# Letting the first gathers of a graph-attention kernel wait for TensorE's table of K and V

## The chip, the cores and the metric

The kernel runs on one core of one Trainium2 chip. The metric is device time in microseconds (us) of one execution. Three runs of the kernel before took 2426.94, 2427.33 and 2434.01 us; their median is 2427.33 us. One more execution was profiled, and every duration below that isn't one of these three is from that profile.

## What is computed

The reference is one layer of graph attention with a residual and a normalization. Nodes N = 6250, edges E = 206250 (sorted by `dst`), D = 128 columns, 8 heads of 16:

```python
Kh, Qh, Vh = x @ WK, x @ WQ, x @ WV            # per node, 8 heads x 16
Eh = edge_attr @ WE                            # per edge
score = einsum('ehd,ehd,ehd->eh', Kh[src], Qh[dst], Eh) / 4
score = exp(clip(score, -5, 5))
wV = segment_sum(Vh[src] * score[:, :, None], dst)
Z = segment_sum(score, dst)
out = layernorm(x + wV / (Z[:, :, None] + 1e-6))
```

All inputs are float32. `Kh[src]` and `Vh[src]` are the costly part: a row of 256 floats for each of 206250 edges, from addresses that only `src` knows.

## The kernel before

The edges are cut into 1612 tiles of 128, and the tiles into 406 batches, nearly all of four tiles. A batch's K and V rows come to SBUF through four indirect DMAs ("gathers", one for each tile, line 314 in `gather`), all issued by GpSimd (POOL). Batches from 12 on (`XB = 12`) gather 1 KB rows of a table `kv` in HBM, which holds K and V of every node. The first twelve don't need this table: they gather the 512-byte rows of `x` itself (48 gathers), and TensorE makes K and V of those rows on the spot (`project`, lines 323 to 335: transposes `xtps`, copies `xgT`, matmuls `kvps`). So the kernel has work while the table is being made. There are 17 buffers for gathered batches (`GB`).

The table is made by `table(b0)`, line 226, called 13 times for groups of four blocks of 128 nodes, 49 blocks in all. For each block TensorE does one float32 matmul of 128x256 (line 232, `kvacc`) into a PSUM bank. Four banks are used in turn, so a block's matmul waits until the block four places ahead has been copied out. The copy to the SBUF tile `kvst` is ScalarE's for even blocks (line 237) and VectorE's for odd ones (line 235). A finished group goes to `kv` in one store of 512 KB on SyncE's queue (line 240); `kvst` has two buffers, so a group's first copies wait for the store of two groups before. The last block of 106 rows has a store of its own (line 245). Every gather from `kv` comes after all of these stores have landed.

Up to batch 11 the instructions of each engine stand where a scheduler put them; from batch 12 on they stand as the loop at line 464 issues them. TensorE's queue holds blocks 0 to 11 of the table, two matmuls of `qrows` (line 258, the table of Q), blocks 12 to 27, one `qrows`, blocks 28 to 35, one `qrows`, blocks 36 to 43, one `qrows`, twelve transposes `xtps` of batches 0 to 2, and blocks 44 to 48; then batch 0 begins (`kvps` line 334, `eps` line 358, `qps` line 354, `pps` line 373, `agg` line 431). Each of these float32 matmuls is two matmul instructions with two weight loads in the trace, so a block of the table is four TensorE records; a transpose is two.

GpSimd's queue holds the 48 gathers of x first and then those of `kv`. Each gather waits for the eighth gather before it (eight semaphores are used in turn) and for its buffer. The first gather of `kv` waits for the stores of the table as well. From batch 16 (`LOCK`) the first gather of batch b also waits for the `qps` matmul of batch b - lag(b), where the lag falls from 12 to 1 within 44 batches and stays there (lines 303 to 320). Batches 0 to 15 have no such wait.

```python
gathered = {b: gather(b) for b in range(min(XB, len(batches)))}   # line 446
for b0 in range(0, NB, KB):                                       # NB = 49, KB = 4
    table(b0)
```

Of the kernel before, what the change touches and what calls it, by code (L numbers as in the profile page):

```python
# [15 lines left out]
P = 128  # L16
# [5 lines left out]
LEFT, RIGHT = 43, 128  # L22
# [6 lines left out]
XB = 12  # L29
# [19 lines left out]
def cut_batches():  # L49
    out, t = [], 0  # L50
    while t < NT:
        k = B
        if t >= NT - TAIL:
            k = 2 if NT - t > 3 else 1
        out.append(range(t, t + k))
        t += k
    return out
# [17 lines left out]
def q_built(j):  # L75

    return min(NB, (j * N // NJ + 3 * P - 1) // P)
# [3 lines left out]
def edge_attention(ctx: ExitStack, tc: tile.TileContext, x, xT, srcT, dstT, dstB, dst0, bnd, lo, eaT,  # L81
                   wq, wkv, we, out, kv, qtab, qs, relD):
    nc = tc.nc
# [6 lines left out]
    wkv_sb = cp.tile([D, 2 * D], F32, name="wkv_sb")  # L90
    nc.scalar.dma_start(wkv_sb, wkv)
    xT_sb = cp.tile([P, XC], F32, name="xT_sb")
# [16 lines left out]
    def src_col(t):  # L109
        return src_sb[0][:, t:t + 1] if t < C0 else src_sb[1][:, t - C0:t - C0 + 1]  # L110

    with ExitStack() as fast:
# [32 lines left out]
        def count(rows, cl, vals, hi):  # L145

            nc.vector.tensor_scalar(cl, vals, 0.0, float(hi), op0=ALU.max, op1=ALU.min)
            nc.vector.tensor_tensor(cl, cl, vals, op=ALU.is_equal)
            nc.vector.tensor_reduce(cn[:rows, len(counts):len(counts) + 1], cl, axis=AX.X, op=ALU.add)
            counts.append(rows)  # L150

        def from_window(i):

            a, k = i * P, min(P, NJ - i * P)
            if i == len(dB_sb):
                dB_sb.append(ip.tile([P, WT * P], I32, name="dB_sb", bufs=1))
                nc.sync.dma_start(dB_sb[i][:k], dstB[a:a + k])
            d = dB_sb[i]
            w = ip.tile([P, 1], F32, name="wq0", bufs=2)
            nc.vector.tensor_tensor(w[:k], d[:k, :1], bnd_c[:k, i:i + 1], op=ALU.min)  # L160
            r = ip.tile([P, WT * P], BF16, name="relq", bufs=1)
            nc.vector.tensor_scalar(r[:k], d[:k], w[:k], None, op0=ALU.subtract)
            nc.sync.dma_start(relD[a:a + k], r[:k])
            cl = wp.tile([P, WT * P], F32, name="clq", tag="kvst", bufs=2)
            count(k, cl[:k], r[:k], QW - 1)
# [52 lines left out]
        def pair_bank(i, name, shape):  # L218

            pool, tag = ((psE, "eps"), (psP, "pps"), (psQ, "qps"), (psP, "pps"))[i % 4]  # L220
            return pool.tile(shape, F32, name=name, tag=tag)


        KB = 4

        def table(b0):
            st = wp.tile([P, KB, 2 * D], F32, name="kvst", bufs=2)
            blocks = range(b0, min(NB, b0 + KB))
            for b in blocks:
                n = min(P, N - b * P)  # L230
                ps = pair_bank(b, "kvacc", [P, 2 * D])
                nc.tensor.matmul(ps[:n], xT_sb[:, LEFT + b * P:LEFT + b * P + n], wkv_sb,
                                 start=True, stop=True)
                if b % 2:
                    nc.vector.tensor_copy(st[:n, b - b0, :], ps[:n])
                else:
                    nc.scalar.copy(st[:n, b - b0, :], ps[:n])
            full = [b for b in blocks if (b + 1) * P <= N]
            if full:
                nc.sync.dma_start(  # L240
                    kv[b0 * P:(b0 + len(full)) * P].rearrange("(b p) f -> p b f", p=P),
                    st[:, :len(full), :])
            if len(full) < len(blocks):
                b = blocks[-1]
                nc.sync.dma_start(kv[b * P:N], st[:N - b * P, b - b0, :])

        batches = cut_batches()
        nbat = len(batches)
# [38 lines left out]
        chunks, aggs, sums, st8, expanded = {}, {}, {}, {}, {}  # L287

        def load_chunk(c):
            if c in chunks or c * CH >= NT:  # L290
                return
            n = min(CH, NT - c * CH) * P
            tl = ep.tile([P, CH * P], F32, name="ea")
            nc.sync.dma_start(tl[:, :n], eaT[:, c * CH * P:c * CH * P + n])
            chunks[c] = tl
# [7 lines left out]
        def lag(b):  # L303

            return max(STEP, 12 - (b - LOCK) // 4)

        def gather(b):
            rows, f = (x, D) if b < XB else (kv, 2 * D)
            g = gp.tile([P, B, 2 * D], F32, name="kvrows")
            for i, t in enumerate(batches[b]):  # L310
                k = min(P, (E - t * P + 63) // 64 * 64)
                if k < P:
                    nc.vector.memset(g[k:, i, :], 0.0)
                ins = nc.gpsimd.indirect_dma_start(  # L314
                    out=g[:k, i, :f], out_offset=None, in_=rows,
                    in_offset=bass.IndirectOffsetOnAxis(ap=src_col(t)[:k], axis=0))
                if i == 0 and b >= LOCK:
                    tc.add_manual_dep(ins.ins, expanded[b - lag(b)].ins.name,
                                      mybir.DependencyInfo(mybir.DependencyClass.Sync, mybir.DependencyReason.DATA),
                                      reason="gathers keep to TensorE's pace")  # L320
            return g
# [96 lines left out]
        def stage_c(b):  # L418
            n, g, oh, m = st8.pop(b)
            for i in range(n):  # L420
# [18 lines left out]
                elif last:  # L439
# [3 lines left out]
                    if k[1] == 0 and k[0] > 0:  # L443
                        ready.append(k[0] - 1)

        gathered = {b: gather(b) for b in range(min(XB, len(batches)))}
        for b0 in range(0, NB, KB):
            table(b0)
            if b0 == 2 * KB:
                load_chunk(0)  # L450
        from_window(0)
        for q in range(q_built(QLOOK + 2)):
            q_rows(q)
# [10 lines left out]
        for b in range(nbat + 4):  # L464
# [6 lines left out]
            if b < nbat:  # L471
                load_chunk(batches[b][0] // CH + EB - 3)
                load_rel(batches[b][0] // RC + 1)
                load_q(batches[b][0] // WT + QLOOK)
                g = gathered.pop(b) if b in gathered else gather(b)
                if b == min(XB, nbat - 1):
                    late_loads()
                if b == min(XB + 8, nbat - 1):
                    relative(C0, NT)
                if b == 14:  # L480
                    from_window(1)
                if b == 0:
                    for i in range(AHEAD):
                        stage_0(i)
                if b > 0:
                    turn(b - 1)
                stage_a(b, g)
            elif b == nbat:
                turn(b - 1)
# [178 lines left out]
```

## Time and profile before

| what | value |
|---|---|
| median of three runs | 2427.33 us |
| the profiled execution's own time | 2430.0 us |
| its span, first to last instruction | 2428.1 us |
| mean granted TensorE clock | 0.811 |
| gathers of x: first starts, last ends | 3.39 us, 63.73 us |
| `kvst` copies of the table: first, last start | 8.4 us, 88.1 us |
| last store of the table is issued | 90.33 us |
| first gather of `kv` | 96.25 us |
| first and last `qps` of batches 0 to 60 | 91.3 us, 413.8 us |

A row of the profile's groups names line, engine, operation and tiles, then the count, busy time and mean duration, then the idle time just before and what ended most of it. In the table of windows each engine's cell is its busy time and, in brackets, the number of its records; PEld is TensorE's weight loads. In a timeline the first two numbers are start and busy time, and the square bracket holds the engine's idle time before the instruction and what ended it. "remote" and "another core or an unknown queue" stand where the profile has no record of what released a wait at that time; there is only one core here.

### The profile page before, as it was taken

To read this page: it belongs to the slowest core of one execution; us is meant where nothing else is said; L and a number is where in the kernel's file an instruction comes from. 1 tells how busy PE (TensorE), PEld (TensorE's weight loads), DVE (VectorE), ACT (ScalarE), POOL (GpSimd) and SP (SyncE) were. 2 spreads that over 40 slices of the span, in tenths; PEclk is the share of its full clock that TensorE was granted. 3 is DMA by queue.
4 is the path that set the end of the run, shared out by engine and by line. 5 is a ranking of instruction groups with operands and counts; after the bars stand their busy time and mean duration, and the time that the engine had idled before them with its cause. 6 is when DMAs were issued, how large, how long until landed. Compare 5 with 4: busy or idle time off the path is not lost.

```text
span 2428.1 us, 24930 instructions
## 1 busy us (share of the span) xinstructions
PE 1539.8 (63%) x6880; PEld 1086.0 (45%) x6880; DVE 1577.4 (65%) x3779; ACT 458.9 (19%) x1572; POOL 1534.0 (63%) x1619
## 2 busy tenths in 40 slices
PE   3587666666665666657666666666666656656665
PEld 2365444444444444444444444444444444444444
DVE  1368778666766666667667666666666667666766
ACT  0232122111111111111111111111111111111111
POOL 7346565666666666666666666666666666666664
PEclk6898898887878888778877878788778788887887
DMA  5645555556554555556456554655555556554642
GB/s 176 201 144 174 179 156 178 165 150 185 170 166 148 168 177 156 164 152 196 147 157 196 160 156 149 184 168 151 169 162 178 147 155 196 157 156 146 197 150 71
DMA packets 178482, 398.16 MB, mean 164 GB/s; under 512 B 61756, under 2 KB 87526, under 8 KB 178336
## 3 DMA queue, kind: packets, MB, share of 16 engines
q0 software_dynamic: 76592, 208.18, 29.4%
q1 hardware_dynamic: 100604, 187.38, 25.2%
q8 instruction: 57, 0.93, 0.2%
q10 hardware_dynamic: 1140, 0.93, 0.1%
q14 instruction: 89, 0.73, 0.1%
HBM read 381.54 MB, written 14.81 MB: 163 GB/s over the span
## 4 chain that ended last, share of the span: by engine, by line
PE 34%; another core or an unknown queue 23%; DVE 19%; issue 16%; ACT 4%; DMA 2%; POOL 1%; DVEq 1%; SPq 0%; ACTq 0%; POOLq 0%
PE agg L431 10%; PE eps L358 10%; PE pps L373 7%; DVE sc L382 4%; DVE kq L379 4%; DVE eq L365 3%; PE qps L354 3%; ACT qT L356 2%; DVE msg L413 2%; PE finps L401 2%; POOL kvrows L314 1%; DVE onehot L340 1%; DVE onehotT L344 1%; DMA kvrows<-kv,src 1%
## 5 line engine op out<-in xcount | busy, mean ns | idle before, releaser
L314 POOL DMA_INDIRECT kvrows<-kv,src x1564 | 1487.1, 951 | 862.3 <-issue 385.6
L431 PEld LDWEIGHTS agg<-msg,onehot 128*128 128x128 f32 x3224 | 516.7, 230 | 664.3 <-issue 520.9
L431 PE MATMUL agg<-msg,onehot 128*128 128x136 f32 x3224 | 560.5, 326 | 352.8 <-DVE msg L413 137.2
L373 PE MATMUL pps<-shift,eq 128*128 128x128 f32 x1612 | 320.5, 332 | 419.6 <-DVE eq L365 238.5
L365 DVE TENSOR_TENSOR eq<-qT,eps 128x512 f32<-128x512 f32 x406 | 276.4, 681 | 476.2 <-ACT qT L356 210.9
L358 PE MATMUL eps<-ea,we_sb 128*128 128x512 f32 (+1 forms) x812 | 528.2, 738 | 16.8 <-issue 13.4
L373 PEld LDWEIGHTS pps<-shift,eq 128*128 128x128 f32 x1612 | 221.4, 168 | 477.4 <-DVE eq L365 282.4
L356 ACT COPY qT<-qps 128x512 f32<-128x512 f32 x406 | 236.8, 583 | 1048.5 <-remote 428.8
L379 DVE TENSOR_TENSOR kq<-kvrows,pps 128x512 f32<-128x512 f32 x406 | 274.8, 677 | 12.1 <-remote 3.5
L413 DVE TENSOR_TENSOR msg<-kvrows,bank 128x512 f32<-128x512 f32 x406 | 274.6, 676 | 9.8 <-ACT bank L391 4.3
L382 DVE TENSOR_REDUCE sc<-kq 128x32 f32<-128x512 f32 x406 | 276.0, 680 | 7.3
L340 DVE TENSOR_TENSOR onehot<-bank,dst_sb 128x512 f32<-128x512 f32 x406 | 275.8, 680 | 0.0
L358 PEld LDWEIGHTS eps<-ea,we_sb 128*128 128x128 f32 x812 | 192.1, 238 | 50.0 <-issue 14.6
L354 PE MATMUL qps<-onehotT,qw 126*128 126x512 bf16 x406 | 187.3, 461 | 0.9 <-ACT qT L356 0.9
L344 DVE TENSOR_SCALAR onehotT<-relb,node 126x512 bf16<-126x512 bf16 x406 | 147.0, 363 | 16.7 <-remote 11.2
L391 ACT ACTIVATE bank<-sc 128x32 f32<-128x32 f32 x406 | 83.0, 204 | 257.2 <-DVE onehot L340 139.8
L401 PEld LDWEIGHTS finps<-sum,shift 128*128 128x128 f32 x478 | 73.1, 215 | 62.4 <-issue 33.9
L401 PE MATMUL finps<-sum,shift 128*128 128x136 f32 x478 | 75.8, 307 | 30.9 <-ACT sum L441 26.2
L262 DVE TENSOR_TENSOR qr<-qrows,qst 128x128 f32<-128x128 f32 (+1 forms) x49 | 14.2, 289 | 116.8 <-ACT qst L261 104.4
L393 ACT ACTIVATE msg<-sc 128x32 f32<-128x32 f32 x406 | 88.0, 217 | 0.0
L385 DVE TENSOR_SCALAR sc<-sc 128x32 f32<-128x32 f32 x406 | 79.2, 195 | 7.3
L441 ACT COPY sum<-agg 128x136 f32<-128x136 f32 x146 | 39.3, 269 | 236.2 <-remote 100.7
(66 smaller groups left out, 525.9 us busy)
## 6 DMA issues: line engine op xcount, KB each, us to landing
ea<-eaT SPq DMA_DIRECT2D x201, 512.0 KB
relb<-relD SPq DMA_DIRECT2D x100, 504.0 KB
kvrows<-kv,src POOLq DMA_INDIRECT x1564
qw<-qs SPq DMA_DIRECT2D x202, 31.5 KB
kv<-kvst SPq DMA_DIRECT2D x12, 512.0 KB
qs<-qst SPq DMA_DIRECT2D x48, 96.0 KB
xb<-x SPq DMA_DIRECT2D x48, 64.0 KB
out<-h SPq DMA_DIRECT2D x48, 64.0 KB
```

The source lines that it names most:

```text
L314: ins = nc.gpsimd.indirect_dma_start(out=g[:k, i, :f], out_offset=None, in_=rows, in_offset=bass.IndirectOffsetOnAxis(ap=src_col(t)[:k], a ...
L340: nc.vector.tensor_tensor(oh[:, :n], iota_p[:, None, :].to_broadcast([P, n, P]), rel[:, t0:t0 + n, None].to_broadcast([P, n, P]), op=ALU.i ...
L354: expanded[b] = nc.tensor.matmul(pq[:, :n * P], loaded[t0 // WT], ohT[:, :n * P], start=True, stop=True)
L356: nc.scalar.copy(qT[:, :n * P], pq[:, :n * P])
L358: nc.tensor.matmul(pe[:, :n * P], we_sb, ea_tiles(t0, n), start=True, stop=True)
L365: nc.vector.tensor_tensor(eq[:, :n * P], qT[:, :n * P], pe[:, :n * P], op=ALU.mult)
L373: nc.tensor.transpose(pp[:, i, :], eq[:, i * P:i * P + P], ident)
L379: nc.vector.tensor_tensor(t1[:, :n], g[:, :n, :D], pp[:, :n], op=ALU.mult)
L382: nc.vector.tensor_reduce(sc[:, :n], t1[:, :n].rearrange("p b (h d) -> p b h d", h=H), axis=AX.X, op=ALU.add)
L401: nc.tensor.matmul(ps, shift[:, P - s:2 * P - s], sums[k], start=i == 0, stop=stop and i == len(parts) - 1)
L413: nc.vector.tensor_tensor(m[:, :n, :D].rearrange("p b (h d) -> p b h d", h=H), g[:, :n, D:].rearrange("p b (h d) -> p b h d", h=H), exp_p[ ...
L431: nc.tensor.matmul(aggs[k], oh[:, i, :], m[:, i, :], start=first and not final, stop=last)
```

## The change

Batches 0 and 1 are gathered ahead of everything as before. The gathers of batches 2 to 11 are now issued between the groups of the table, and the first of a batch's four gathers waits for TensorE's matmul of the last block of one group:

```diff
-                nc.tensor.matmul(ps[:n], xT_sb[...], wkv_sb, start=True, stop=True)
+                made = nc.tensor.matmul(ps[:n], xT_sb[...], wkv_sb, start=True, stop=True)
...
+            return made
...
-        def gather(b):
+        def gather(b, made=None):
...
                 if i == 0 and b >= LOCK:
-                    tc.add_manual_dep(ins.ins, expanded[b - lag(b)].ins.name,
+                    made = expanded[b - lag(b)]
+                if i == 0 and made is not None:
+                    tc.add_manual_dep(ins.ins, made.ins.name,
...
-        gathered = {b: gather(b) for b in range(min(XB, len(batches)))}
+        gathered = {b: gather(b) for b in range(2)}
         for b0 in range(0, NB, KB):
-            table(b0)
+            made = table(b0)
             if b0 == 2 * KB:
                 load_chunk(0)
+            for b in range(len(gathered), min(XB, nbat)):
+                if (b - 2 if b < 5 else b) * KB > b0:
+                    break
+                gathered[b] = gather(b, made=made)
```

Worked out from the condition, and the same in the semaphore counts of the built program: batches 2, 3 and 4 wait for blocks 3, 7 and 11 (groups 0, 1 and 2); batches 5 to 11 wait for blocks 23, 27, 31, 35, 39, 43 and 47 (groups 5 to 11).

The first gather of a batch in the code is not the first in the built queue everywhere. Up to batch 4 it is. In batches 5 to 11 the scheduler put the other three gathers of the batch ahead of it, so the wait stands at the batch's fourth gather. Counted from 0 through GpSimd's queue, the waits are at gathers 8, 12, 16, and then 23, 27, 31, 35, 39, 43 and 47, which is the last gather of x. The instructions of every engine are the same in kind and number; on the other engines their order is the same too, and only the names of some of the gathers' eight semaphores that they wait for differ.

More of the change, by code (lines that the diff above doesn't have):

```diff
@@ L231, in table @@
                 ps = pair_bank(b, "kvacc", [P, 2 * D])
-                nc.tensor.matmul(ps[:n], xT_sb[:, LEFT + b * P:LEFT + b * P + n], wkv_sb,
-                                 start=True, stop=True)
+                made = nc.tensor.matmul(ps[:n], xT_sb[:, LEFT + b * P:LEFT + b * P + n], wkv_sb,
+                                        start=True, stop=True)
                 if b % 2:
@@ L444, in stage_c @@
                         ready.append(k[0] - 1)
-        gathered = {b: gather(b) for b in range(min(XB, len(batches)))}
+        gathered = {b: gather(b) for b in range(2)}
         for b0 in range(0, NB, KB):
-            table(b0)
+            made = table(b0)
             if b0 == 2 * KB:
                 load_chunk(0)
+            for b in range(len(gathered), min(XB, nbat)):
+                if (b - 2 if b < 5 else b) * KB > b0:
+                    break
+                gathered[b] = gather(b, made=made)
+        assert len(gathered) == min(XB, nbat)
         from_window(0)
```

## The prediction

> **What bounds the kernel now.** I read the page first.
>
> ```profile
> span 2428.1 us, 24930 instructions
> PE 1539.8 (63%) x6880; PEld 1086.0 (45%) x6880; DVE 1577.4 (65%) x3779; ACT 458.9 (19%) x1572; POOL 1534.0 (63%) x1619
> PE 34%; another core or an unknown queue 23%; DVE 19%; issue 16%; ACT 4%; DMA 2%; POOL 1%; DVEq 1%; SPq 0%; ACTq 0%; POOLq 0%
> ```
>
> No engine is full, and 23% of the chain that ended last lies on releases that the profile can't name. So I looked at the start, which is all that the change touches, in the timeline of GpSimd:
>
> ```profile
> 3.39 1.11 POOL L314 DMA_INDIRECT kvrows<-x,src  x1 [1.82 <-DMA src<-srcT]
> ...
> 27.77 0.94 POOL L314 DMA_INDIRECT kvrows<-x,src  x1 [0.31 <-issue]
> ...
> 62.78 0.95 POOL L314 DMA_INDIRECT kvrows<-x,src  x1 [0.31 <-issue]
> 96.25 0.95 POOL L314 DMA_INDIRECT kvrows<-kv,src  x1 [32.51 <-DMA relb<-relD]
> ```
>
> The 48 gathers of x run without a gap, one every 1.25 us, and then GpSimd is idle for 32.51 us until the table has landed. The table is what is late. ScalarE's timeline (every second block) shows why:
>
> ```profile
> 42.10 0.37 ACT L237 COPY kvst<-kvacc 128x256 f32<-128x256 f32 x1 [8.73 <-remote]
> 53.31 0.37 ACT L237 COPY kvst<-kvacc 128x256 f32<-128x256 f32 x1 [10.83 <-remote]
> 64.50 0.37 ACT L237 COPY kvst<-kvacc 128x256 f32<-128x256 f32 x1 [10.82 <-remote]
> ...
> 70.85 0.65 ACT L237 COPY kvst<-kvacc 128x256 f32<-128x256 f32 x2 [1.18 <-PE qrows L258]
> ```
>
> VectorE's copies lie between these (47.70, 58.96, 68.71), so a block takes 5.6 us, though a copy lasts 0.37 to 0.42 us. Blocks 24 to 48, copied from 70.85 to 88.1, take 0.72 us each. The windows put numbers to both:
>
> ```profile
> core 0: us, PE busy (x) PEld busy (x) DVE busy (x) ACT busy (x) POOL busy (x), PEclk, DMA share, GB/s
> 3.40:19.20 15.80, 10.11 (x29) 7.40 (x29) 7.17 (x21) 3.61 (x9) 12.14 (x13) 0.89 1.02 359
> 19.20:70.80 51.60, 16.07 (x34) 7.59 (x34) 3.84 (x11) 2.88 (x9) 33.86 (x36) 0.58 0.34 99
> 70.80:88.10 17.30, 14.35 (x61) 11.24 (x60) 6.76 (x20) 6.75 (x20) 0.00 (x0) 0.88 0.82 262
> 96.20:105.00 8.80, 5.32 (x29) 3.71 (x28) 4.65 (x11) 2.57 (x7) 6.63 (x7) 1.00 1.04 306
> 105.00:117.40 12.40, 2.81 (x16) 1.89 (x13) 2.17 (x4) 0.35 (x1) 8.54 (x9) 0.80 0.81 246
> ```
>
> The reader is to see two things. In the slow stage (second row) the DMA engines are only 0.34 busy, so the stores aren't short of bandwidth. And TensorE stalls twice in the same way: GpSimd gathers without a pause, TensorE puts through 58 records (29 + 29, first row) or 57 (29 + 28, fourth row) at full pace, and from then on its completions trickle: 5.6 us for a block of four records is 1.4 us a record. The stall ends soon after the gathers pause. The same is seen later, in the chain of waits,
>
> ```profile
> 218.70 7.19 another core or an unknown queue
> ```
>
> which ends at 225.89, in a pause of GpSimd:
>
> ```profile
> 226.10 0.94 POOL L314 DMA_INDIRECT kvrows<-kv,src  x1 [2.14 <-remote]
> ```
>
> I read this as: unbroken gathers hold back TensorE's completions after some 57 records, and a pause frees them. What the carrier is, no view shows. The release comes 1.9 us after the last gather ends here (223.96); after the long run of x's gathers (63.73) it comes 5.0 to 7.1 us later (copies at 68.71 and 70.85).
>
> **The change, part by part.** Nothing is added or removed but ten waits on GpSimd, and one gather in each of seven batches goes behind its three fellows. Behind each wait stand all later gathers, those of `kv` among them, and behind those every batch. I count gathers from 0, in the queue's order.
>
> *Gathers 8, 12, 16* (batches 2 to 4) started at 14.01, 19.01 and 24.02. In TensorE's timeline a row of `kvacc` matmuls ends with block 6 at 11.28 (5.82 + 5.46), the next with block 11 at 17.65 (13.75 + 3.90); block 7 is copied at 15.01. All three waits are met before they are asked: cost nothing. Gathers 20, 21, 22 have no wait, so all stays as before until gather 22 ends at 32.46.
>
> *Gather 23* waits for block 23. There GpSimd pauses for the first time. TensorE's release: 1.9 us by the short run, 5.0 to 7.1 by the run of 48. A run of 23 lies between, nearer to the short one (8 to 11 gathers); I take 3: 35.5. Then blocks 16 to 19, multiplied already, are copied and 20 to 23 multiplied: 2 us. Gather 23 starts at 37.5 (36.5 to 41.5). GpSimd has lost 5 us; but block 23 is there at 37.5, where before it was copied at 68.71.
>
> *Gathers 23 to 38* then run in one go, 16 x 1.25 = 20 us, to 57.5, if their waits are met. TensorE goes at 0.72 us a block for 57 records: blocks 24 to 27 (16), `qrows` (4), blocks 28 to 35 (32), block 36 (4): until 37.5 + 13 x 0.72 = 47. So blocks 27, 31 and 35 are in time for gathers 27 (42.5), 31 (47.5) and 35 (52.5). Block 39 isn't for gather 39 at 57.5: three blocks at 5.6 us would make it 64.
>
> *Gathers 39 to 46*: second pause at 57.5, release after 2.5 us, block 39 half a microsecond later; gather 39 at 60.5. TensorE has 57 records again: blocks 40 to 43 and `qrows` (20), twelve transposes (24), blocks 44 to 46 (12). Block 43 is done by 63.5, so gather 43 isn't held, and the run ends at 70.5.
>
> *Gather 47* meets block 47 in the trickle: third pause, release at 73, end of x's rows at 74.2. Waits in all 5 + 3 + 2.5 = 10.5 us. Block 48 is copied at about 73.9.
>
> *The first gather of `kv`* came 8.15 us after block 48's copy began (88.1 to 96.25: SyncE's queue took 2.2 us, the landing most of the rest). Kept, that is 82, and GpSimd is free at 74.2. So `kv`'s gathers start at 82 instead of 96.25: 14 us sooner. Bounds: with no second throttle GpSimd alone decides, 37.5 + 25 x 1.25 = 69 (27 us); with every release at 7 us the three pauses end at 41.5, 69 and 86, and `kv` starts at 95 (1 us). That upper end is the row of a run of 48, and these are of 23, 16 and 8, so I stay near the short one.
>
> *What follows* is the same work in the same order, gated batch by batch by TensorE, so I carry the shift to the end one for one. Before, TensorE ran free for 17 us around the start of batch 0 (88.1 to 105); now from 73 to 82 and on for 57 records, beside one lone gather: no charge, or 3 us if it is short. Net 14: 2430.0 - 14 = 2416 for an execution like the profiled one, whose time lies 2.7 above the median, so 2413 for the median.
>
> [...]
>
> **Rivals.** *(A) The gathers aren't what holds the table.* If the 5.6 us come from something else (the wait of `kvst` for its stores, the load of x), block 47 still comes at about 86, gather 47 runs to 87 and is hidden before 96.25: 2427. For it: no view names the carrier, and a group's first copies do wait for stores. Against it: the 58 and 57 records, and the end of both stalls with the gathers.
>
> *(B) Lockstep, slower.* Each of the seven waits from gather 23 on could find its group not done, because the gathers just ahead throttled it: pause, a release of 5.0 to 7.1 us, then four blocks, 2.9 us; 9 us each, 63 in all. GpSimd would end x's rows at 63.7 + 63 = 127 and `kv` would start 31 us later than now: 2458. It decides for slower once the waits sum to over 32.5 us (96.25 - 63.73). Against it: after each release TensorE has 57 records free, some twelve blocks, so a wait comes once in three or four groups.
>
> *(C) Given back in part.* x's and `kv`'s gathers follow each other closer, and the releases are longer than mine: half of the 14 us is lost, 2420.
>
> **How the numbers follow.** Main case (`kv` from 78 to 87): 0.5, 2409 to 2418. More (`kv` from 69 to 78): 0.15, 2400 to 2409. C: 0.13, 2418 to 2425. A: 0.13, 2427. B: 0.09, 2440 to 2460. The range 2401 to 2425 holds the first three cases. A measurement of this kernel can tell some 0.3% (7.3 us) from no change, so faster means under 2420: main, more, and a third of C, 0.69. Same: A and the rest of C, 0.22. Slower: 0.09.
>
> **What would show it.** GpSimd's timeline: 23 gathers to 32.5, a first pause that ends between 36 and 42, a second near 57, a third near 71 before x's last gather, and the first gather of `kv` near 82 after a pause of some 8 us, not 32.51. `kvst` copies at under 1 us a block between 36 and 47. The last copy near 74. If copies stay at 5.6 us with GpSimd idle, A holds; if GpSimd waits at each of the seven, B does; if `kv` starts near 82 but the end moves by less than 8 us, C does. The prediction also fails if the pace of the later batches (5.92 us each: 2331.9 us from 96.25 to the end, over 394) changes by itself; 1% of that would hide all.

## The result and the profile after

Six runs of the changed kernel took 2412.46 to 2416.43 us, median 2414.45; six of the kernel before 2422.07 to 2434.01, median 2427.14. The ratio is 0.9947, 95% interval 0.993 to 0.9965: 12.7 us less. The profiled execution took 2414.75 us, 15.3 less than the profiled one of before.

The page's first lines and its chain, after:

```profile
span 2413.0 us, 24940 instructions
PE 1537.5 (64%) x6880; PEld 1091.4 (45%) x6880; DVE 1575.8 (65%) x3779; ACT 456.6 (19%) x1572; POOL 1530.8 (63%) x1619
PE 33%; another core or an unknown queue 22%; DVE 22%; issue 15%; ACT 4%; DMA 1%; POOL 1%; DVEq 0%; SPq 0%; ACTq 0%; POOLq 0%
```

The mix is close to that of before, as most of the 406 batches are untouched. GpSimd's timeline holds the change (first number the start; in brackets its idle time and what ended it):

```profile
3.42 1.11 POOL L315 DMA_INDIRECT kvrows<-x,src  x1 [1.85 <-DMA src<-srcT]
...
31.14 0.94 POOL L315 DMA_INDIRECT kvrows<-x,src  x1 [0.30 <-issue]
40.61 0.94 POOL L315 DMA_INDIRECT kvrows<-x,src  x1 [8.52 <-PE kvacc L232]
...
67.57 0.94 POOL L315 DMA_INDIRECT kvrows<-x,src  x1 [2.30 <-remote]
...
78.00 0.94 POOL L315 DMA_INDIRECT kvrows<-x,src  x1 [5.75 <-PE kvacc L232]
88.12 0.94 POOL L315 DMA_INDIRECT kvrows<-kv,src  x1 [9.17 <-DMA qw<-qs]
```

Three pauses, and then `kv` 8.1 us sooner than at 96.25. The pauses stand before gathers 23, 43 and 47, with 23, 20 and 4 gathers in one go ahead of them. ScalarE's copies of the table, as before every second block:

```profile
27.38 0.37 ACT L237 COPY kvst<-kvacc 128x256 f32<-128x256 f32 x1 [7.54 <-remote]
34.38 0.37 ACT L237 COPY kvst<-kvacc 128x256 f32<-128x256 f32 x1 [6.63 <-remote]
35.84 0.65 ACT L237 COPY kvst<-kvacc 128x256 f32<-128x256 f32 x2 [1.08 <-remote]
39.33 0.37 ACT L237 COPY kvst<-kvacc 128x256 f32<-128x256 f32 x1 [2.84 <-DMA kv<-kvst]
...
79.55 0.38 ACT L237 COPY kvst<-kvacc 106x256 f32<-106x256 f32 x1
```

These are blocks 12, 14, then 16 and 18 together, 20, and at last 48. Block 14 in the trace of before, and TensorE's row of blocks 19 to 27 after:

```profile
27.41 0.37 ACT L237 COPY kvst<-kvacc 128x256 f32<-128x256 f32 x1 [4.53 <-remote]
```

```profile
36.27 5.79 PE L232 MATMUL kvacc<-wkv_sb,xT_sb 128*128 128x256 f32 x18 [0.25 <-DVE kvst L235]
```

The trickle ends at 35.8, 3.7 us after gather 22 has ended (32.1). Until then TensorE was further behind than in the trace of before, though nothing had changed yet: block 14 was copied at 34.38 instead of 27.41. The windows (columns as in the prediction):

```profile
core 0: us, PE busy (x) PEld busy (x) DVE busy (x) ACT busy (x) POOL busy (x), PEclk, DMA share, GB/s
...
19.20:33.00 13.80, 6.21 (x14) 3.53 (x13) 1.54 (x5) 1.01 (x3) 9.84 (x11) 0.62 0.43 136
33.00:41.00 8.00, 5.95 (x16) 4.45 (x17) 2.22 (x6) 1.99 (x6) 0.39 (x1) 0.59 0.48 167
41.00:47.00 6.00, 5.47 (x25) 4.21 (x24) 2.39 (x7) 2.06 (x7) 4.48 (x6) 1.00 0.90 269
47.00:53.00 6.00, 3.77 (x10) 3.05 (x11) 2.35 (x7) 1.56 (x5) 4.57 (x5) 0.74 0.94 314
53.00:60.00 7.00, 2.34 (x11) 1.46 (x9) 0.91 (x3) 0.30 (x1) 5.38 (x6) 0.98 0.70 214
60.00:67.00 7.00, 0.00 (x0) 0.00 (x0) 0.42 (x1) 0.00 (x0) 4.05 (x5) 0.51 0.22 57
```

From 41 to 47 TensorE goes at full pace beside gathers (49 records in 6 us); then the pace drops, and in the last row it has no record at all. The chain has that stretch as its longest piece:

```profile
55.66 14.45 issue
70.10 1.11 PE xtps L330 x4
```

Between 41.00 and 55.66 there are some 90 records (45 of matmuls and 44 of weight loads up to 60.00). The last block in time was block 39, copied at 54.04; counted from block 24 on, that is 72 records (16 blocks of four and two `qrows` of four). Such a count depends on where it ends: up to where TensorE stands still, the run-up to the second stall of before has 81 records (25 of them after 105.00, by their starts, up to 109.4), not 57.

### The profile page after: what moved, and what is told of

The parts are those of the page before. It is cut to its first block, busy times and chain, and to the rows that moved or that the text cites. A ratio compares the mean times of both kernels' runs of the same rounds, so it can differ in the third digit from the quotient of the medians.

```text
span 2413.0 us, 24940 instructions
## 1 busy us (share of the span) xinstructions
PE 1537.5 (64%) x6880; PEld 1091.4 (45%) x6880; DVE 1575.8 (65%) x3779; ACT 456.6 (19%) x1572; POOL 1530.8 (63%) x1619
## 2 busy tenths in 40 slices
DMA packets 178482, 398.16 MB, mean 165 GB/s; under 512 B 61756, under 2 KB 87526, under 8 KB 178336
## 4 chain that ended last, share of the span: by engine, by line
PE 33%; another core or an unknown queue 22%; DVE 22%; issue 15%; ACT 4%; DMA 1%; POOL 1%; DVEq 0%; SPq 0%; ACTq 0%; POOLq 0%
PE eps L361 10%; PE agg L434 9%; PE pps L376 7%; DVE sc L385 5%; DVE kq L382 4%; DVE eq L368 4%; PE qps L357 3%; DVE msg L416 3%; ACT qT L359 2%; DVE onehot L343 2%; PE finps L404 2%; DVE onehotT L347 1%; POOL kvrows L315 1%; DVE sc L388 1%
## 5 line engine op out<-in xcount | busy, mean ns | idle before, releaser
L315 POOL DMA_INDIRECT kvrows<-kv,src x1564 | 1484.3, 949 | 834.9 <-issue 386.4
L347 DVE TENSOR_SCALAR onehotT<-relb,node 126x512 bf16<-126x512 bf16 x406 | 144.7, 357 | 17.5 <-remote 11.2
L404 PEld LDWEIGHTS finps<-sum,shift 128*128 128x128 f32 x478 | 79.2, 232 | 52.8 <-issue 37.3
L404 PE MATMUL finps<-sum,shift 128*128 128x136 f32 x478 | 81.1, 324 | 19.9 <-ACT sum L444 14.3
L263 DVE TENSOR_TENSOR qr<-qrows,qst 128x128 f32<-128x128 f32 (+1 forms) x49 | 14.1, 289 | 94.2 <-ACT qst L262 76.8
```

Of the source, the lines that this page charges most:

```text
L315: ins = nc.gpsimd.indirect_dma_start(out=g[:k, i, :f], out_offset=None, in_=rows, in_offset=bass.IndirectOffsetOnAxis(ap=src_col(t)[:k], a ...
L404: nc.tensor.matmul(ps, shift[:, P - s:2 * P - s], sums[k], start=i == 0, stop=stop and i == len(parts) - 1)
```

## The experiments

The theory: indirect gathers without a break hold TensorE's completions back; a pause frees them; so pauses while the table is being made buy time. Rival A: something else holds the table. Further rivals: a fixed count of 57 records after each pause; and, for the later batches, that pauses don't matter because TensorE has a pace of its own.

The kernels ran in four sets, each set on one chip with the kernel before beside it. The chips differ: the kernel before took 2450.16 us (one run), 2043.42, 2426.63 and 2425.35 us (medians of 27, 17 and 9 runs) on them. So times are compared within a set. The first set has one run of each kernel, while runs of one kernel on one chip spread by up to some 20 us in the others; so its argument rests on the traces. The only traces of the kernel before are from the first comparison and from the second set, so a start of `kv` that is set against 96.25 may be a comparison between chips.

### First set: what holds the table, and what one wait does

*Plain loads on GpSimd's queue.* The kernel before, with x's gathers turned into loads of consecutive rows (batches 0 to 11, which so get other rows):

```diff
-                ins = nc.gpsimd.indirect_dma_start(out=g[:k, i, :f], ..., in_=rows, in_offset=...)
+                if b < XB:
+                    ins = nc.gpsimd.dma_start(g[:k, i, :f], x[t * P:t * P + k])
+                else:
+                    ins = nc.gpsimd.indirect_dma_start(...)
```

> The kernel before, with the 48 gathers of x replaced by plain loads of as many consecutive rows of x, still issued by GpSimd one tile at a time (so the first twelve batches get the wrong rows). Theory G (GpSimd's unbroken issue of gathers holds TensorE back, by what it does or by the bytes it asks for): if it is any DMA that GpSimd issues, the stall stays, 4 to 6 us a block between 22 and 65 us, first kv gather near 96; if it is the indirect addressing, the table runs free at 0.7 to 1 us a block and is copied by 45, with the first kv gather at 64 to 70, where GpSimd is free. Rival A (the stores of the table or the load of x hold it): the table is copied at 88 as before, kv at 96.

*Plain loads on SyncE's queue*, one for each of the twelve batches:

```diff
+            if b < XB:
+                nc.sync.dma_start(g[:, :n, :D], x[t0 * P:(t0 + n) * P].rearrange("(b p) f -> p b f", p=P))
+                return g
```

> The kernel before, with the 48 gathers of x replaced by twelve plain loads of consecutive rows on SyncE's queue, one for each batch, the same bytes (so the first twelve batches get the wrong rows). GpSimd issues nothing before the kv gathers. Theory G: no stall at all in the table stage, blocks at 0.7 to 1 us, last copy at 45 to 55, first kv gather at 53 to 63, end 30 to 45 us sooner. Rival A (stores, loads, anything but the gathers): last copy still near 88, or later since the loads stand ahead of stores on SyncE's queue.

They took 2409.67 and 2411.35 us, beside 2450.16. The stage of the table with plain loads from GpSimd, and the first gather of `kv`:

```profile
19.20:53.30 34.10, 24.38 (x101) 18.79 (x100) 11.88 (x34) 10.61 (x32) 12.19 (x23) 0.95 0.84 278
```

```profile
61.82 1.00 POOL L317 DMA_INDIRECT kvrows<-kv,src  x1 [28.44 <-DMA ea<-eaT]
```

GpSimd issued 23 loads in this stage, the last by 33.4, at a DMA share of 0.84, and TensorE put through 201 records; in the kernel before, 68 in 51.6 us beside 36 gathers. The last copy is at 53.2 (56.2 with SyncE's loads, `kv` at 63.01): no stall, though the last copies came 8 and 1 us later than expected. Rival A falls, and the bytes don't hold TensorE either: what does comes with GpSimd's gathers. Whether it is the indirect addressing or a long row on GpSimd is not fully separated. The longest row of plain loads took 8.7 us (16 loads, 24.6 to 33.4), about as long as the gathers had run before the second stall (8.8 us), and less than before the first (15.8 us).

*Half the records.* The kernel before, with the table's matmuls on bf16 halves, so that a block is two records instead of four (K and V of the table are rounded):

```diff
+        xT_h, wkv_h = (t.bitcast(BF16).rearrange("p (c h) -> p c h", h=2)[:, :, 1] for t in (xT_sb, wkv_sb))
-                nc.tensor.matmul(ps[:n], xT_sb[...], wkv_sb, start=True, stop=True)
+                nc.tensor.matmul(ps[:n], xT_h[...], wkv_h, start=True, stop=True)
```

> The kernel before, with the table's matmuls on the upper halves of x and the weights as bf16 (K and V are rounded): one matmul and one weight load a block, two TensorE records instead of four. Theory R (TensorE may put through some 57 records beside unbroken gathers and then one per 1.4 us): the stall begins after some 26 blocks instead of 15, and a stalled block takes 2.8 us instead of 5.6; last copy near 75, kv near 83. Theory T (TensorE is held after some 15 us of x's gathers, whatever it did until then): the stall begins at 19 to 22 us as before; blocks then 2.8 us if the trickle goes by records (last copy near 80, kv near 88), 5.6 if it goes by matmuls (kv near 96).

TensorE's timeline, well into the 48 gathers:

```profile
50.94 0.37 PE L233 MATMUL kvacc<-wkv_sb,xT_sb 128*128 128x256 bf16 x1 [7.27 <-issue]
53.80 0.37 PE L233 MATMUL kvacc<-wkv_sb,xT_sb 128*128 128x256 bf16 x1 [2.49 <-issue]
56.54 0.37 PE L233 MATMUL kvacc<-wkv_sb,xT_sb 128*128 128x256 bf16 x1 [2.38 <-issue]
```

Blocks are 2.7 to 2.9 us apart at the core of the stall (some 2.0, some 3.6) instead of 5.6, 1.4 us a record once more: the trickle goes by records. It began near 24 us, after some 20 blocks. With 57 records free it would have begun after 26 blocks; from a fixed time, at 19 to 22. So neither fits exactly. `kv` started at 88.18, and the time was 2434.87 us.

*One wait of the ten* (batch 5's alone):

```diff
-                gathered[b] = gather(b, made=made)
+                gathered[b] = gather(b, made=made if b == 5 else None)
```

> The changed kernel with one of its ten waits kept, that of batch 5 at gather 23 for block 23; the other nine are left out. Theory G: the first pause is as in the changed kernel, gathers 23 to 47 then run in one go to about 72 and hold TensorE from about 55 on; release at 74 to 78, last copy near 83 to 86, kv near 91 to 95, so 3 to 7 us later than with all ten waits, and 1 to 5 sooner than before. If the first pause carried the whole gain, kv would start at 88 or sooner. Rival A: kv at 96.

```profile
41.01 0.94 POOL L315 DMA_INDIRECT kvrows<-x,src  x1 [8.80 <-PE kvacc L232]
...
93.81 0.95 POOL L315 DMA_INDIRECT kvrows<-kv,src  x1 [21.83 <-DMA ea<-eaT]
```

The first pause is the same as in the changed kernel, the copies run freely to 54, and then the 25 gathers in one go hold TensorE again (copies at 56.7, 65.2, 74.2, 78.7). `kv` is 2.4 us sooner than in the trace of before (from the first comparison): the first pause alone is worth about that, the other 5.7 us come with the later waits. The one run took 2448.21 us, which can't be told from 2450.16.

### Second set: a chip without the stall

The changed kernel again, the kernel before for a trace, and x's gathers in runs of eight, without and with waits for `kv`'s first four batches:

```diff
-                if i == 0 and made is not None:
+                if made is not None and (i == 0 or b < XB):
...
-                if (b - 2 if b < 5 else b) * KB > b0:
+                if (3 * (b // 2) - 1) * KB > b0 and b0 < 11 * KB:
```

```diff
-            return max(STEP, 12 - (b - LOCK) // 4)
+            return 9 if b < LOCK else max(STEP, 12 - (b - LOCK) // 4)
...
-                if i == 0 and b >= LOCK:
+                if i == 0 and b >= XB:
```

> The changed kernel once more, unaltered, beside the kernel before on the same chip, as the measure for the next two. Both theories: 0.4 to 0.7% under the kernel before; kv's first gather at about 88 us; pauses of x's gathers near 32 to 41, 65 to 67 and 72 to 78 us.

> The kernel before once more, for a trace on this chip: kv's first gather at 96 us (94 to 98), the last copy of the table near 88, and the end within 8 us of the other runs of this kernel.

> x's gathers in runs of eight: gathers 8, 16, 24 and 32 wait for blocks 11, 23, 35 and 47 of the table. Theory (a run of some 12 unbroken gathers, about 15 us, is what begins to hold TensorE; a run of eight seldom does): block 11 is copied near 17 us, 23 near 27, 35 near 37, 47 near 48 and the last one near 50 to 56; x's rows end at 66 to 76; kv's gathers start there, at 70 to 78 instead of 88. If the lead is carried whole or a little more, the end is 10 to 17 us under the changed kernel; but kv's sixteen gathers now follow x's without a pause, TensorE is held in the first batches, and then 2 to 10 us of it remain. Rival (57 records at full pace whatever the pauses, then 1.4 us a record): pauses of this length don't help, block 35 is late by 10 us or more, the table ends at 75 or later and kv starts at 85 or later, with an end within 5 us of the changed kernel's.

> As the kernel with runs of eight, and besides kv's first four batches after x's (12 to 15) each wait for the expansion of batches 3 to 6, as later batches wait for theirs. Theory: the run of gathers at the change from x to kv is broken, TensorE's first batches are not held, the copy of batch 8's second product comes 3 to 8 us sooner than in the run without these waits, and the end is 0 to 8 us under it. Rival (the start of kv's gathers alone sets the end): batches 12 to 15 come later by the waits, and the end is the same within 3 us or later.

None of the four came out as expected, since on this chip nothing stalls. The kernel before on it, in GpSimd's timeline, the window of the table, the chain and the group of the gathers:

```profile
62.66 0.94 POOL L314 DMA_INDIRECT kvrows<-x,src  x1 [0.30 <-issue]
63.90 0.95 POOL L314 DMA_INDIRECT kvrows<-kv,src  x1 [0.30 <-issue]
```

```profile
19.20:49.10 29.90, 21.31 (x91) 16.28 (x89) 10.31 (x28) 9.35 (x28) 22.58 (x25) 0.94 0.91 293
```

```profile
DMA 34%; DVE 28%; POOL 16%; issue 12%; PE 8%; DVEq 0%; ACT 0%; SPq 0%; POOLq 0%; ACTq 0%
...
L314 POOL DMA_INDIRECT kvrows<-kv,src x1564 | 1483.7, 949 | 476.4 <-issue 363.4
```

180 records beside 25 gathers: TensorE takes no notice of them, the table ends at 49.1, ahead of x's last gather, and `kv` follows without a pause. Nothing "unknown" is left in the chain. GpSimd sets the end: 1612 gathers at 1.25 us are 2015 us of the 2043. On such a chip the ten waits are met before they are asked (no pause of x's gathers in the trace), and the change is worth nothing: 2043.59 against 2043.42 us, ratio 1.0001 (0.9992 to 1.001). The runs of eight do wait here (pauses of 2.75 and 2.56 us), `kv` starts 4.7 us later (68.61), and the end is 4.1 us later: 1.002 (1.0011 to 1.0029); with `kv`'s waits 1.0026 (1.0017 to 1.0036). This agrees with the theory: without the stall, no gain. Why this chip has no stall isn't shown.

### Third set: runs of eight, where there is a stall

> The same kernel with x's gathers in runs of eight, once more. If this chip lets TensorE go on under gathers (the kernel before at about 2043 us, kv's first gather at 64 us in it), nothing new: 0.1 to 0.3% over the kernel before. If gathers hold TensorE here (the kernel before at 2420 to 2450 us, its kv's first gather at 96 us): theory, kv's first gather at 70 to 78 us, and the end 12 to 30 us under the kernel before, a ratio of 0.988 to 0.995 against the changed kernel's 0.9947; rival (57 records at full pace whatever the pauses), kv's first gather at 85 us or later and a ratio of 0.993 or more.

> The same with waits for kv's first four batches too, on the same chip. Without a hold: as the run before it, within 2 us. With the hold: theory (the unbroken run at the change from x to kv costs TensorE its first batches), 0 to 8 us under the run without these waits; rival (only kv's start counts), the same within 3 us or later.

Runs of eight, GpSimd's timeline:

```profile
26.95 0.94 POOL L315 DMA_INDIRECT kvrows<-x,src  x1 [0.47 <-PE kvacc L232]
...
43.11 0.95 POOL L315 DMA_INDIRECT kvrows<-x,src  x1 [6.48 <-PE kvacc L232]
...
54.74 0.94 POOL L315 DMA_INDIRECT kvrows<-x,src  x1 [1.93 <-PE kvps L337]
...
75.37 0.95 POOL L315 DMA_INDIRECT kvrows<-kv,src  x1 [0.30 <-issue]
```

The second wait costs 0.17 us beyond the usual gap, so gathers 8 to 23 run as one row of 16, and TensorE is held once (copies at 27.8, 31.7, 37.3). The last copy comes at 55.2, and `kv` starts at 75.37 with no gap after x. The time is 2409.15 against 2426.63 us, ratio 0.9936 (0.991 to 0.9961). That is what the theory gave, and the rival's 85 us for `kv` is refuted. Against 96.25 in the first comparison `kv` starts 21 us sooner, and the end is 17.5 us sooner than that of the kernel before on this chip. In the row of 32 gathers that begins at 54.74 TensorE pays (it has no record from 76.8 on):

```profile
86.73 1.09 PE L376 MATMUL pps<-shift,eq 128*128 128x128 f32 x4 [9.92 <-issue]
```

With waits at `kv`'s first batches too, the time is 2414.22 us, ratio 0.9951 (0.9933 to 0.9969), with `kv` at 78.67. No gain, as the rival had it: TensorE stalls later, in a row of 24 gathers that begins at 97.98 and after which GpSimd waits 14.57 us for `qps`. Neither ratio can be told from the changed kernel's 0.9947, and neither is shown to beat it.

### Fourth set: breaks throughout

If long rows of gathers were what costs, breaks would pay in all 394 later batches. The changed kernel, with a small write on GpSimd after each batch's gathers, and with three after every second batch:

```diff
+            if b >= XB:
+                for _ in range(1):
+                    nc.gpsimd.iota(io_i, pattern=[[1, 3 * P]], base=-P, channel_multiplier=-1)
             return g
```

```diff
+            if b >= XB and b % 2:
+                for _ in range(3):
+                    nc.gpsimd.iota(io_i, pattern=[[1, 3 * P]], base=-P, channel_multiplier=-1)
             return g
```

> The changed kernel, and from batch 12 on GpSimd writes one small constant tile again after each batch's four gathers (128x384 int32, 0.40 us by the gap between two such rows at the start of the trace): a short pause after every run of four. Nothing else computes differently. If gathers hold TensorE on this chip (the kernel before at 2410 to 2450 us): by the theory that it is the unbroken run that holds TensorE, and that 0.4 us are enough of a break, the stalls go and GpSimd sets the pace, 5.0 + 0.4 us a batch: 88 + 394 x 5.4 + 10 = 2226 us, 2215 to 2260. If a break has to be as long as the pauses seen so far (the release came 1.9 us after the last gather), 0.4 us change nothing, runs still go on until a wait stops them, and the time stays at 2390 to 2430. Rival (TensorE's own pace, or a count of its records, sets 5.9 us a batch, and pauses don't matter): 2414, or up to 165 us more where the writes add to it. If gathers don't hold TensorE here (2043 us): 2043 + 394 x 0.4 = 2200.

> The same with a longer pause after every second batch: three such writes, 1.2 us after a run of eight gathers. With the hold: by the theory, and 1.2 us being enough of a break, 11.2 us for two batches, 88 + 197 x 11.2 + 10 = 2304 us, 2295 to 2340. If 1.2 us are too short: 2390 to 2430, or more. Rival (TensorE's own pace): 2414 to 2640. If gathers don't hold TensorE here: 2043 + 197 x 1.2 = 2280.

They took 2398.72 us, ratio 0.989 (0.9849 to 0.9931), and 2404.89 us, 0.9915 (0.9885 to 0.9945): near the changed kernel's 0.9947 (0.993 to 0.9965) and nowhere near 2226 or 2304. The short breaks may have gained some 0.5% more; the intervals just touch, and the changed kernel wasn't run on this chip. GpSimd's groups in the changed kernel, with the short breaks, and with the long ones (the number after the bar is busy time, the one after the second bar idle time, of which "issue" is the gap between two gathers):

```profile
L315 POOL DMA_INDIRECT kvrows<-kv,src x1564 | 1484.3, 949 | 834.9 <-issue 386.4 <-remote 229.9 <-PE qps L357 55.5
```

```profile
L315 POOL DMA_INDIRECT kvrows<-kv,src x1564 | 1486.9, 951 | 626.9 <-issue 395.4 <-remote 108.4 <-PE qps L360 33.5
L326 POOL IOTA io_i<- 128x384 int32 x394 | 184.4, 468 | 3.1
```

```profile
L315 POOL DMA_INDIRECT kvrows<-kv,src x1564 | 1482.8, 948 | 536.0 <-issue 408.8 <-remote 39.3 <-PE qps L360 26.7
L326 POOL IOTA io_i<- 128x384 int32 x591 | 271.0, 458 | 28.3
```

Idle time that isn't "issue", plus the writes: 834.9 - 386.4 = 449 us; 626.9 - 395.4 + 184.4 + 3.1 = 419; 536.0 - 408.8 + 271.0 + 28.3 = 426. GpSimd is kept from gathering for nearly the same time however it is cut (within 7%): most of the writes only took the place of waits. On the chips that stall, the mean distance between the first gathers of batches 112 and 392 is 5.79 to 5.89 us a batch in all ten traces, rows of 4, 8 or 12 alike; on the other it is 5.01 in all four. So in the later batches the length of a row of gathers hardly mattered: a batch took some 0.8 us more there, whatever the row. "A short break ends it" is refuted; the rival, that pauses don't matter, came nearest. But the breaks, of 0.47 us and 3 x 0.46 us, are shorter than the 1.9 us of the release that the prediction read from the trace, so what a break of that length would do to these batches is untested. Whether TensorE needs that much time without gathers, can't go faster beside them, or is slower there for another reason (its mean granted clock was 0.811 before, 0.885 on the chip without the stall), these runs don't tell apart.

## Why the prediction was right, and where it wasn't

- **That unbroken gathers are what holds the table, and pauses free it: right for the table's stage.** Shown by the plain loads (no gathers, no stall: 201 records in 34.10 us) and by the copies after the first pause; on the chip without the stall the waits gained nothing (2043.59 against 2043.42 us). For the later batches it doesn't carry over: short breaks after every four gathers left their pace at 5.79 us a batch. Nor does it hold on every chip: on that of the second set TensorE didn't slow beside gathers (180 records in 29.9 us beside 25 of them); on that of the first comparison it did (68 in 51.6 us beside 36).
- **Gathers 8, 12 and 16 cost nothing; gather 22 ends at 32.46:** right (32.08, no pause). That "all stays as before" until then held for GpSimd, not for TensorE, which was further behind (block 14 at 34.38, not 27.41).
- **"Gather 23 starts at 37.5":** too early, 40.61, inside the bounds of 36.5 to 41.5. The release took 3.7 us, near the 3 taken. The failed term is the "2 us" for blocks 16 to 23: it was 4.8 us (35.84 to 40.61). Block 19 was still to be multiplied too, and TensorE did it and the next four in one row from 36.27 on, at some 0.8 us a block and a granted clock of 0.59. ScalarE's 2.84 us of waiting for the store of an earlier group lay beside that and cost nothing here: the gather waits for the matmul of block 23, not for a copy, and TensorE's row has no gap.
- **"57 records" at full pace after a pause: wrong.** By the count up to the last block in time it was 72. So block 39 came in time (54.0), gather 39 didn't wait, and no second pause came at 57.5. The row of gathers became 20 long instead of 16, and TensorE stood from 55.66 to 70.10. The 58 and 57 rest on where the prediction ended its windows (19.20 and 105.00): TensorE started 14 and 25 more records before it stood still. Its sums also leave out the `qrows` after block 35, and count one after block 43, which the description of TensorE's queue has too and neither trace shows. What sets the number stays open. **"1.4 us a record" inside a stall: right**, and with half the records a block it was 1.4 again.
- **Waits of 10.5 us in all, x's rows to 74.2, `kv` at 82:** 8.5 + 2.3 + 5.8 = 16.6 us, 78.94, and 88.12. The step from the last copy to `kv` was right: 8.57 us against 8.15. So the start gained 8.1 us, not 14, and lies just outside the main case's 78 to 87. For the start, rival C (longer releases) is nearer.
- **"I carry the shift to the end one for one": it holds roughly.** From 93.81 over 88.18 to 61.82 for `kv`'s start, the ends in the first set are 2446.3, 2433.0 and 2407.8: 5.6 us at the start went with 13.3 at the end, the next 26.4 with 25.2, each from one run.
- **The time: right, in part by luck, as two errors offset each other.** In the profiled executions the start gave 8.1 us and the later batches the other 7.0: 2331.9 us from `kv`'s first gather to the end before, 2324.9 after, 5.918 and 5.901 us a batch. The prediction had 14 and 0. It named this as what could hide all. Whether the 7 us belong to the change is open: runs of the kernel before spread by 12 us, the traces of different kernels by 0.1 us a batch, and no run ties this to the waits. On the medians 12.7 us were gained.
- **Rivals.** A is refuted. B (lockstep) didn't come: three pauses, 16.6 of the 32.5 us that GpSimd was idle before `kv`. On the chip without the stall GpSimd has no such idle time behind x's rows (`kv` at 63.90, x's last gather at 62.66), and there runs of eight delayed `kv` by 4.7 us and the end by 4.1.

What carries the stall stays open. No view names it, and the same program shows it on some chips and not on another one (the last copy of the table began at 88.1 us in the first comparison, at 49.09 in the second set). It went by trace records, 1.4 us each with four a block and with two. Every run that is listed with a granted clock was recorded, so whether the stall, and with it the gain, is there without recording is open too.

## What to carry to other kernels

When two engines stall together in a trace, take the suspect's work away in kind (the same bytes without indirect addressing) before you gate it: that separates cause from coincidence, if the substitute comes in rows as long. A wait put on an engine that has slack moves its pause to where it is useful: here 16.6 us of waits stood ahead of 32.5 us of idle time, and `kv` started 8.1 us sooner. On the chip where the slack wasn't there, the waits of the runs of eight cost nearly their full length (4.1 of 4.7 us). So try such a change on more than one chip. A count that appears twice in one trace (58, 57) is no rule until a run with another rhythm has shown it, and it must be ended by the same event each time; and a total that comes out right doesn't prove its terms, so check the first event that the change moves (here `kv`'s first gather) before the end.

## What the runs showed that wasn't expected

- The same kernel takes 2425 to 2450 us in three sets and in the first comparison, and 2043 on the chip of the second set, with the same DMA traffic (398.16 MB) and a gather every 1.25 us on both. Nearly all of the 384 us are pauses of GpSimd's gathers: beyond 1.25 us each, 362 us from `kv`'s first gather to its last before, 5 us on that chip; the rest is `kv`'s later start (96.25 against 63.90). The mean granted clock was 0.811 and 0.885.
- A plain load of 128 rows from GpSimd's queue took 0.53 to 0.56 us within a row of loads, an indirect gather of as many rows came every 1.25 us.
